# Second moments of h2: two products of 64 by 65 sums in place of one of 128 by 129

## The chip, the core and the metric

The program runs on one NeuronCore of a Trainium2 chip. The metric is the time of one execution on the device in microseconds (us). TensorE multiplies, VectorE, ScalarE and GpSimd work element by element, SyncE issues most transfers. TensorE is an array of 128 rows (the contraction) by 128 columns (the outputs of one pass), which can also be used in halves of 64 columns.

## What is computed

Two layers on x of shape (4, 256, 64, 64), in fp32. The first makes 49 weights for each pixel by a dilated 7x7 convolution and a 1x1 convolution, takes their softmax, and sums the 49 shifted copies of x with them. The second is a bottleneck block, with batch statistics in each normalisation:

```python
residual = x
h = relu(bn(conv(x, w1), g1, b1))            # 1x1, 256 -> 64 channels
h = relu(bn(conv(h, w2, pad=1), g2, b2))     # 3x3,  64 -> 64 channels: "h2"
h = bn(conv(h, w3), g3, b3)                  # 1x1,  64 -> 256 channels
return relu(h + residual)
```

The third normalisation needs mean and variance of each of 256 channels of conv(h2, w3). They follow from the sums of h2 over all pixels and from the sums of products of each two of its 64 channels (the second moments): the variance of channel c is w3_c' M w3_c less the square of the mean. Only these 64 by 64 sums and 64 plain sums are wanted.

## The kernel before

The kernel makes the weights of the first layer in transformed form (to about 450 us of the span), then turns them into banded matrices and applies them to x on TensorE, writing the result y to memory (`y_dram`) and taking conv1's statistics on the way (line 785 is conv1). Next come the 3x3 convolution (lines 952 and 964), the part that is changed here, and the output stage.

**h2 in SBUF.** `h2` has 128 partitions: 64 channels of one group of pixels in partitions 0 to 63 (the half with a = 0), the same channels of another group in 64 to 127. It is cut into 16 blocks of 128 partitions by 512 columns.

**The loop over blocks** (lines 1021 to 1036). For each block:
- ScalarE applies scale, shift and relu in place (line 1023).
- TensorE transposes it in four pieces j of 128 columns (line 1026) into a PSUM tile `pturn`, so that pixels lie on partitions.
- VectorE copies the tile (line 1028) into one of three buffers `ht`, each of four pieces of 129 columns. The 129th column holds ones, written once by GpSimd (line 1001).
- TensorE multiplies each piece by itself (line 1030): stationary operand 128 columns, moving operand all 129, summed in the PSUM tile `moments` over all 64 pieces. An fp32 product is done in two passes, so that the profile shows 128 matmuls with a weight load each.

Of the 128 by 129 sums, the two diagonal blocks of 64 by 64 (one for each half) and the last column (the plain sums) are used; the blocks that pair one half with the other are not read.

**After the loop.** Two VectorE copies take the diagonal blocks into `prod` (line 1046), one instruction scales the sums (line 1047), and a product with w3 (line 1049) with a few small steps (lines 1050 to 1059) gives scale and shift for the output. In the output stage TensorE computes conv3 (line 1013), VectorE adds y (line 1070), ScalarE applies the relu (line 1075), and SyncE's queue writes the result.

**Order.** The stages up to conv1 have hand-written orders on some engines; the loop here has none, and a scheduler orders each engine's instructions from its own estimates. It puts TensorE's work as: 4 transposes, 4 products of block 0, and then five times 12 transposes and 12 products, three blocks at a time, as many as `ht` has buffers. VectorE and ScalarE take their blocks in order. PSUM has 8 tiles in the pool `pb`, of which `moments` holds one.

Of the kernel before, what the change touches and what calls it, by code (L numbers as in the profile page):

```python
# [44 lines left out]
ALU = mybir.AluOpType  # L45
# [3 lines left out]
P = 128  # L49
B, C, H, W = 4, 256, 64, 64  # L50
# [5 lines left out]
MID = 64  # L56
# [37 lines left out]
def conv_seq_kernel(ctx: ExitStack, tc: tile.TileContext, xp, xt, w1, b1, w2t, b2, m1t, g1, be1,  # L94
                    m2t, g2, be2, m3t, g3, be3, z, mask, pavg, out, ydram):
    nc = tc.nc
    def pool(stack, name, bufs, space=None, **kw):
        if space is not None:
            kw["space"] = space
        return stack.enter_context(tc.tile_pool(name=name, bufs=bufs, **kw))  # L100
# [396 lines left out]
    for g in range(2):  # L497
        half = slice(g * MID, (g + 1) * MID)
# [7 lines left out]
    outer = pool(ctx, "outerp", 1).tile([P, OUTER], F32, name="outer")  # L506
# [155 lines left out]
    o = 4 * XT  # L662
# [3 lines left out]
    o = OUTER - NH1  # L666
# [33 lines left out]
    o = NH1  # L700
# [3 lines left out]
    o = 7 * C * 4  # L704
# [123 lines left out]
    def small(*shape):  # L828
        o, n = n_small[0], 1
        for d in shape:  # L830
            n *= d
        n_small[0] += n
        assert n_small[0] <= ARENA
        t = arena[:, o : o + n]
        return t.rearrange("p (n v) -> p n v", v=shape[1]) if len(shape) > 1 else t
# [159 lines left out]
    ops = [outer[:, 2048 * i : 2048 * (i + 1)].rearrange("p (r w) -> p r w", w=W) for i in range(4)]  # L995
    o = 4 * 2048

    ht = [outer[:, o + 4 * (P + 1) * i : o + 4 * (P + 1) * (i + 1)].rearrange("p (j c) -> p j c", j=4) for i in range(3)]
    o += 12 * (P + 1)
    for t in ht:  # L1000
        nc.gpsimd.memset(t[:, :, P:], 1.0)
    yins += [outer[:, o + 1024 * i : o + 1024 * (i + 1)] for i in range(6)]
    yins += [arena[:, 1024 * i : 1024 * (i + 1)] for i in range(7)]
    for n in range(19, len(parts)):
# [14 lines left out]
    moments = pb_.tile([P, 512], F32, tag="pb", name="moments")  # L1019
    blocks = [(slot, i, q) for slot in range(2) for i in range(2) for q in range(Q)]  # L1020
    for n, (slot, i, q) in enumerate(blocks):
        v = h2[:, slot, q, 512 * i : 512 * (i + 1)]
        nc.scalar.activation(v, v, AF.Relu, bias=sh2, scale=sc2)
        pt = pb_.tile([P, 512], F32, tag="pb", name="pturn2")
        for j in range(4):
            nc.tensor.transpose(pt[:, j * P : (j + 1) * P], v[:, j * P : (j + 1) * P], ident)  # L1026
        t = ht[n % 3]
        nc.vector.tensor_copy(t[:, :, :P], pt.rearrange("p (j c) -> p j c", j=4))
        for j in range(4):
            nc.tensor.matmul(  # L1030
                moments[:, : P + 1],
                t[:, j, :P],
                t[:, j, :],
                start=(n == 0 and j == 0),
                stop=(n == len(blocks) - 1 and j == 3),
            )
    prod = small(MID)
    sums = small(1)
    w3p = small(C)[:MID]
# [1 line left out]
    mv3 = small(NH, 2)  # L1041
    sq3 = small(NH, 1)
    nc.gpsimd.memset(one, 1.0 / (B * H * W))
    for g in range(2):
        half = slice(g * MID, (g + 1) * MID)
        nc.vector.tensor_copy(prod[half], moments[half, half])
    nc.vector.tensor_scalar(sums, moments[:, P : P + 1], 1.0 / (B * H * W), None, ALU.mult)
    pt = pb_.tile([P, 512], F32, tag="pb", name="pprod")
    nc.tensor.matmul(pt[:MID, :C], prod, w3m, start=True, stop=True)
    nc.vector.tensor_tensor(w3p, pt[:MID, :C], w3m[:MID], ALU.mult)  # L1050
# [1 line left out]
    for half in range(NH):  # L1052
        c = slice(half * P, (half + 1) * P)
# [8 lines left out]
    blocks = [(slot + 2 * g, i, half) for slot in range(2) for i in range(2) for half in range(NH) for g in range(2)]  # L1062
    for k, (b, i, half) in enumerate(blocks):
        o = ops[k % 4]

        n = 256 if k in (0, len(blocks) - 1) else 512
# [68 lines left out]
```

## Time and profile before

| what | value |
| --- | --- |
| median of 3 runs | 800.9 us (800.84 to 802.21) |
| profiled execution: its time, its span | 799.53 us, 797.6 us |
| TensorE, VectorE, ScalarE, GpSimd busy, of the span | 91%, 72%, 37%, 9% |
| granted TensorE clock, mean | 0.971 |
| products of line 1030: number, busy | 128, 16.7 us |
| transposes of line 1026: number, busy | 64, 9.4 us |
| copies of line 1028: number, busy | 16, 10.2 us |
| relus of line 1023: number, busy | 16, 11.4 us |
| first and last product of the moments start at | 720.7 us, 744.1 us |

Busy time counts an engine as busy from the start of an instruction to its end; matmuls overlap, so what one of them takes of TensorE is read from the spacing of their starts. "PEld" is the weight load that goes ahead of each matmul. In a row of the profile, 128*64 after the operation means 128 rows and 64 columns of the array, and 128x512 the partitions and elements of the operand.

### The profile page before, as it was taken

The page shows a single profiled execution, that of the slowest core. Times are in us where ns is not written, and L with a number is a line of the kernel's source. Part 1 is how long each engine was busy: PE and PEld are TensorE (multiplying, and loading weights), DVE is VectorE, ACT ScalarE, POOL GpSimd, SP SyncE. Part 2 cuts the span into 40 slices and gives each one's busy share as a digit, 9 for nine tenths or more (in the row PEclk, how much of TensorE's full clock was granted, in tenths as well). Part 3 has the DMA queues.
Part 4 walks back from the last instruction along what each step waited for, and adds up shares of the span by engine and source line. Part 5 has one row for each costly group of instructions (what it writes and reads, how often), then busy time and mean ns, then how long its engine had stood idle before and what let it go on. Part 6 is the DMA issues. An engine that isn't in the chain of part 4 may idle for free.

```text
span 797.6 us, 10675 instructions
## 1 busy us (share of the span) xinstructions
PE 729.1 (91%) x4080; PEld 590.2 (74%) x4080; DVE 574.6 (72%) x682; ACT 297.7 (37%) x594; POOL 75.7 (9%) x143
## 2 busy tenths in 40 slices
PE   0949999999999999988999999999999979979996
PEld 0938977888888888867888888988887854438742
DVE  4489989999666999999999867233341337663697
ACT  4640155112551101110111158434442446345497
POOL 3210010001000020000002113222222200000000
PEclk9979999999999999998999999999999998998997
DMA  7941089913898886210210013666766669361298
GB/s 290 373 162 41 0 292 297 382 57 126 287 341 349 311 307 233 71 41 11 60 37 16 2 57 101 202 220 212 229 234 212 212 238 342 108 196 39 85 391 367
DMA packets 59236, 150.24 MB, mean 188 GB/s; under 512 B 7346, under 2 KB 35634, under 8 KB 55090
## 3 DMA queue, kind: packets, MB, share of 16 engines
q1 hardware_dynamic: 51216, 141.11, 49.7%
q10 hardware_dynamic: 7970, 8.45, 3.0%
q8 instruction: 32, 0.52, 0.3%
q14 instruction: 18, 0.15, 0.1%
HBM read 93.81 MB, written 55.74 MB: 188 GB/s over the span
## 4 chain that ended last, share of the span: by engine, by line
PE 72%; DVE 15%; ACT 5%; DMA 4%; issue 2%; POOL 0%; SPq 0%; ACTq 0%; DVEq 0%; POOLq 0%
PE acc L262 42%; PE acc L752 13%; DVE arena L151 9%; PE acc L785 4%; PE pconv L964 3%; PE pdirect L952 3%; DVE arena L1070 3%; PE acc L566 2%; PE moments L1030 2%; PE acc L325 2%; ACT outer L1075 1%; DMA outer<-in_xt_dram 1%; ACT arena L573 1%; DMA w1raw<-in_w_dram 1%; PE pturn L1026 1%
## 5 line engine op out<-in xcount | busy, mean ns | idle before, releaser
L262 PE MATMUL acc<-arena 128*128 128x343 f32 (+3 forms) x2000 | 380.2, 353 | 20.5 <-DVE arena L151 20.5
L262 PEld LDWEIGHTS acc<-arena 128*128 128x128 f32 x2000 | 321.6, 192 | 78.1 <-issue 15.7
L151 DVE SCALAR_TENSOR_TENSOR arena<-arena 128x1024 f32<-128x1024 f32 (+7 forms) x192 | 290.5, 1554 | 24.7 <-PE acc L262 14.2
L752 PEld LDWEIGHTS acc<-arena,outer 128*128 128x128 f32 x1024 | 116.0, 193 | 11.3 <-issue 10.1
L752 PE MATMUL acc<-arena,outer 128*128 128x128 f32 x1024 | 118.8, 277 | 3.1 <-issue 2.9
L793 DVE BATCH_NORM_STATS2 st<-acc 128x6 f32<-128x512 f32 x16 | 11.2, 699 | 68.2 <-PE acc L785 68.0
L286 ACT COPY sv<-acc 128x392 f32<-128x392 f32 x40 | 19.1, 484 | 99.2 <-PE acc L262 87.3
L170 ACT COPY stage<-raw 128x128 f32<-128x128 f32 x128 | 43.6, 415 | 23.9 <-DMA raw<-in_xp_dram 23.5
L325 PE MATMUL acc<-powers,w1raw 128*128 128x196 f32 (+1 forms) x196 | 45.3, 394 | 6.6 <-DMA w1raw<-in_w_dram 5.0
L325 PEld LDWEIGHTS acc<-powers,w1raw 128*128 128x128 f32 x196 | 44.5, 314 | 7.1 <-issue 7.0
L590 ACT COPY outer<-acc 128x784 f32<-128x784 f32 x8 | 6.5, 812 | 101.8 <-PE acc L262 101.8
L1013 PE MATMUL pconv<-arena,w3m 64*128 64x512 f32 (+1 forms) x144 | 43.0, 587 | 0.6 <-DVE arena L1070 0.6
L123 ACT COPY outer<-outer 64x2048 f32<-64x2048 f32 x15 | 28.4, 1895 | 38.4 <-DMA outer<-in_xt_dram 38.4
L151 DVE SCALAR_TENSOR_TENSOR outer<-outer 128x784 f32<-128x784 f32 (+2 forms) x47 | 36.8, 835 | 3.6 <-ACT outer L906 3.6
L1013 PEld LDWEIGHTS pconv<-arena,w3m 64*128 64x128 f32 x144 | 20.7, 185 | 21.9 <-DVE arena L1070 16.0
L1075 ACT ACTIVATE outer<-arena 128x512 f32<-128x512 f32 (+1 forms) x58 | 34.7, 695 | 1.3 <-DVE arena L849 1.1
L773 DVE COPY bks<-acc 128x256 f32<-128x256 f32 x32 | 11.3, 417 | 32.5 <-PE acc L752 32.5
L1070 DVE SCALAR_TENSOR_TENSOR arena<-pconv,arena 128x512 f32<-128x512 f32 (+1 forms) x58 | 34.3, 667 | 0.0
L124 POOL COPY outer<-outer 64x1792 f32<-64x1792 f32 x15 | 25.1, 1676 | 95.5 <-DMA outer<-in_xt_dram 80.1
L607 ACT COPY acc<-bks 128x392 f32<-128x392 f32 x40 | 18.5, 488 | 40.7 <-DVE outer L592 33.8
L573 ACT COPY arena<-acc 128x512 f32<-128x512 f32 x52 | 27.1, 708 | 14.8 <-PE acc L566 14.4
L964 PE MATMUL pconv<-outer,arena 128*128 128x512 f32 x72 | 31.1, 592 | 0.0
(143 smaller groups left out, 627.7 us busy)
## 6 DMA issues: line engine op xcount, KB each, us to landing
raw<-in_xp_dram SPq DMA_DIRECT2D x36, 608.0 KB, 5.3
outer<-in_xt_dram SPq DMA_DIRECT2D x17, 896.0 KB, 6.3
out_dram<-outer SPq DMA_DIRECT2D x14, 1024.0 KB, 4.5
arena<-y_dram SPq DMA_DIRECT2D x25, 512.0 KB, 7.9
fsort_dram<-stage SPq DMA_DIRECT2D x2, 4864.0 KB, 14.7
arena<-fsort_dram SPq DMA_DIRECT2D x8, 1216.0 KB, 10.0
y_dram<-outer SPq DMA_DIRECT2D x16, 512.0 KB, 5.4
aside_dram<-sv ACTq DMA_DIRECT2D x40, 196.0 KB, 5.7
```

Of the source, the lines that this page charges most:

```text
L123: nc.scalar.copy(t[:MID], x[MID:])
L151: nc.vector.scalar_tensor_tensor(out, in0, scalar, in1, ALU.mult, ALU.add)
L170: (last if last and k + a == 2 else nc.scalar.copy)(d[:, k, :, PLACE[b], 2 * a : 2 * a + 2, i : i + count], raw[:, lo : lo + 4 * count - 3 ...
L262: nc.tensor.matmul(acc[i][d][:, o : o + (hi - lo) * K], xi[:, i, CW * w : CW * w + CW, :].rearrange("p x t -> p (x t)"), u[i][:, lo * K : ...
L325: nc.tensor.matmul(pw[:, o : o + n], w1raw[:, :, u * K7 + v], powers[:, u, :n], start=(u == 0), stop=(u == K7 - 1), skip_group_check=True,)
L573: nc.scalar.copy(dst, src)
L752: nc.tensor.matmul(dst[:, :: NT - 1] if edge else pts[c][:, o : o + 128], x[:, i, half * P : (half + 1) * P], amat[:, b % 2, :, c, blocks, ...
L785: nc.tensor.matmul(pt[a * MID : (a + 1) * MID, :], w1m[:, n, :], ys[a, n][:, 512 * i : 512 * i + 512], start=(n == 0), stop=(n == NH - 1), ...
L964: nc.tensor.matmul(m[k], wu[:, k, j, :], vs[k][:, g, j : j + R, :], start=(j == 0), stop=(j == 1))
L1013: nc.tensor.matmul(pt[:, :n], w3m[part, half * P : (half + 1) * P], h2[part, slot, q, lo : lo + n], start=True, stop=True)
L1070: nc.vector.scalar_tensor_tensor(v, conv3(b, q, i, half, lo, n), sc3[:, half : half + 1], v, ALU.mult, ALU.add)
L1075: nc.scalar.activation(dst, v.rearrange("p (r w) -> p r w", w=R), AF.Relu, bias=sh3[:, half : half + 1])
```

## The change

Each piece of `ht` is cut into two groups g of 64 columns with a column of ones each (4 pieces of 2 by 65 columns in place of 4 by 129). For each piece and group there is one product: the group's 64 columns are the stationary operand, its 65 the moving one, and the sums go to the 64 partitions of `moments` that belong to the group, which is one half of the array's columns. The sums are then 128 by 65: the diagonal blocks lie one below the other, the plain sums in column 64, and one copy takes them. The products double in number, from 64 to 128 (from 128 passes to 256).

```diff
-    ht = [outer[:, o + 4 * (P + 1) * i : o + 4 * (P + 1) * (i + 1)].rearrange("p (j c) -> p j c", j=4) for i in range(3)]
-    o += 12 * (P + 1)
+    HT = 8 * (MID + 1)
+    ht = [outer[:, o + HT * i : o + HT * (i + 1)].rearrange("p (j g c) -> p j g c", j=4, g=2) for i in range(3)]
+    o += 3 * HT
     for t in ht:
-        nc.gpsimd.memset(t[:, :, P:], 1.0)
+        nc.gpsimd.memset(t[:, :, :, MID:], 1.0)
...
         t = ht[n % 3]
-        nc.vector.tensor_copy(t[:, :, :P], pt.rearrange("p (j c) -> p j c", j=4))
+        nc.vector.tensor_copy(t[:, :, :, :MID], pt.rearrange("p (j g c) -> p j g c", j=4, g=2))
         for j in range(4):
-            nc.tensor.matmul(
-                moments[:, : P + 1],
-                t[:, j, :P],
-                t[:, j, :],
-                start=(n == 0 and j == 0),
-                stop=(n == len(blocks) - 1 and j == 3),
-            )
+            for g in range(2):
+                nc.tensor.matmul(
+                    moments[g * MID : (g + 1) * MID, : MID + 1],
+                    t[:, j, g, :MID],
+                    t[:, j, g, :],
+                    start=(n == 0 and j == 0),
+                    stop=(n == len(blocks) - 1 and j == 3),
+                    skip_group_check=True,
+                )
...
-    for g in range(2):
-        half = slice(g * MID, (g + 1) * MID)
-        nc.vector.tensor_copy(prod[half], moments[half, half])
-    nc.vector.tensor_scalar(sums, moments[:, P : P + 1], 1.0 / (B * H * W), None, ALU.mult)
+    nc.vector.tensor_copy(prod, moments[:, :MID])
+    nc.vector.tensor_scalar(sums, moments[:, MID : MID + 1], 1.0 / (B * H * W), None, ALU.mult)
```

## The prediction

> **What bounds the kernel now.** I read the chain of work that ended last first, in the stretch from the normalisation of h2 to the output stage, since the change touches only the loop over the 16 blocks there. Columns: start in us, length in us, what.
>
> ```profile
> 720.73 2.09 PE moments L1030 x8
> 722.81 2.20 PE pturn L1026 x12
> 725.01 2.68 PE moments L1030 x24
> 727.69 1.31 PE pturn L1026 x12
> 729.00 2.86 PE moments L1030 x24
> 731.86 1.31 PE pturn L1026 x12
> ...
> 741.50 2.87 PE moments L1030 x24
> ```
>
> TensorE alone carries this stretch. After one block by itself the order is three blocks of transposes (12 instructions), then the three products (24: an fp32 product of j is two passes, 64 products give 128 records). One turn is 731.86 - 727.69 = 4.17 us: 1.31 of transposes (109 ns each), 2.68 of products (112 ns each, as in the third row) and 0.18 of waiting. The last turn ends at 744.37. The groups of the same stretch say what one instruction costs and how idle the others are:
>
> ```profile
> L1030 PE MATMUL moments<-outer 128*128 128x129 f32 x128 | 16.7, 288 | 0.9 <-DVE outer L1028 0.9
> L1030 PEld LDWEIGHTS moments<-outer 128*128 128x128 f32 x128 | 15.6, 199 | 1.9 <-DVE outer L1028 1.3
> L1028 DVE COPY outer<-pturn 128x512 f32<-128x512 f32 x16 | 10.2, 685 | 14.5 <-PE pturn L1026 14.5
> L1046 DVE COPY arena<-moments 64x64 f32<-64x64 f32 x2 | 0.4, 223 | 1.9 <-PE moments L1030 1.8
> ```
>
> VectorE has 0.685 us a block and idles 14.5 us; ScalarE's 16 relus end at 729.3. The view of busy time by stretches adds the clock and what lies behind:
>
> ```profile
> 718.70:724.50 5.80, 4.89 (x21) 4.49 (x22) 1.38 (x2) 5.80 (x10) 0.00 (x0) 0.50 0.19 74
> 724.50:744.40 19.90, 19.86 (x173) 19.07 (x171) 8.83 (x15) 4.79 (x7) 0.00 (x0) 1.00 0.01 1
> 744.40:751.10 6.70, 5.54 (x34) 4.22 (x36) 4.29 (x17) 2.04 (x6) 0.00 (x0) 1.00 0.00 0
> 751.10:779.10 28.00, 28.00 (x92) 12.98 (x88) 28.00 (x45) 27.84 (x44) 0.00 (x0) 1.00 0.89 360
> ```
>
> Busy time is PE, weight loads, VectorE, ScalarE, GpSimd; then clock, DMA share, GB/s. TensorE runs at half clock up to 724.50. The queues are empty (share 0.01) from then to 751, so no transfer waits inside this stage, and the output stage behind it starts from its results: what the stage gives up reaches the end.
>
> **Does the array run two half-width products at once?** The timeline of line 785, whose products write 64 array columns each in alternate halves, answers:
>
> ```profile
> 519.77 0.59 PE L785 MATMUL acc<-outer,w1m 128*64 128x512 f32 x1
> 519.78 0.59 PE L785 MATMUL acc<-arena,w1m 128*64 128x512 f32 x1
> 520.20 0.59 PE L785 MATMUL acc<-outer,w1m 128*64 128x512 f32 x1
> 520.21 0.59 PE L785 MATMUL acc<-arena,w1m 128*64 128x512 f32 x1
> 520.73 0.49 PE L752 MATMUL acc<-arena,outer 128*128 128x128 f32 x2
> ```
>
> The halves start within 10 ns of each other, and each starts again 0.43 us later for 512 columns: 0.84 ns a column in both at once. The last row prices the return to the full array: 520.73 - 520.20 = 0.53, of which 0.43 is streaming, so about 97 ns pass before the next weight load begins. The way in, from line 752 at 647.35 to line 785's first load at 647.56, is 0.204 for 128 columns (0.107): 97 ns too.
>
> **What the Trainium skill says.** (1) TensorEngine Tiling (Array Packing), Key Properties: tiles load and multiply in parallel, and changing the tiling mode drains the engine. The trace agrees with both, and the drain is 97 ns here. (2) TensorE: Matmul & The Clock Gate, LDWEIGHTS: the load goes with the number of columns, P/1.2 ns. Line 785's 64-column loads take 139 ns against 192 for 128 in line 1030: 53 less, as stated. (3) Same page, Back-to-back issue gap: a floor of about 25 ns from start to start, 62 ns per matmul with hardware decode off. No run here shows so small a matmul, but lines 1030's 109 to 112 ns for a load and a matmul rule out 62 for each of the two. (4) Same page, The HAM clock gate: the clock follows activity in free-running windows of 3.4 us. The trace agrees: half clock ended at 724.50, after a window that was busy throughout.
>
> **The change, part by part.** The view of instruction order adds one thing that the diff doesn't show: the turn becomes M8 T1 M16 T3 T4 T4 (M products, 8 to a block; T transposes). One transpose of the next block slips in between the products, four times over.
>
> *Product.* A block has 16 passes, 8 in each half. A pass is 65 x 0.84 = 54 ns; line 1030 takes 112 for 129 x 0.84 = 108, so I add 4: **58 ns**. Its load (64 columns, 54 ns) hides under the pass before, as in line 785. A block: 8 x 58 = 0.46 us against 8 x 112 = 0.90. Bounds: not below 54; from above, two passes in turn, 116. The queue must take 32 instructions in 0.46 us, 14 ns each. The densest evidence is three pairs of semaphore instructions of the transposes, each pair 125 ns apart with 8 instructions between: 16 ns at most, some 9 when the 51 ns of the first is taken off. So 58 stands, with 70 possible.
>
> *Switches.* Into products: drain 97 + an uncovered load of 54 = 0.15 us. Back: 97 + 107 = 0.20. A turn has two of each.
>
> *A turn.* Products of the first block at 0 to 0.46; switch 0.20, one transpose 0.11, switch 0.15: 0.93. Two blocks to 1.86. VectorE's copies for them end about 0.55 and 1.24, so they hold nothing up. Switch 0.20, three transposes 0.33, eight 0.87: 3.26. Then either the switch (0.15) or VectorE's copy: in the trace 1.055 us pass from a block's last transpose (727.86) to its product's load (728.91), which gives 3.39. So **3.41 against 4.17: 0.76 less**, four times: 3.0. The old 0.18 of waiting has gone into the drain.
>
> *Start.* Block 0 is done about 0.45 us sooner, but the 12 transposes after it then run nearly all at half clock (218 ns), where now the last few run after 724.50 at 109. The next products begin at 724.78 instead of 724.85: 0.1 less.
>
> *End.* Three blocks follow the last transposes with no slot to fill, and VectorE is next in line: its third copy ends 1.24 after the first product, load at 1.30, product to 1.82. With the switch, 2.08 after the last transpose starts (741.24), against 744.19 - 741.24 = 2.95 now: 0.87 less.
>
> *Around it.* One copy of 128x64 for two of 64x64 (0.22 + 0.24): 0.23 less. Three GpSimd memsets of 8 columns for 4 (105 ns each, over by 714.7, five us ahead of the first copy), the copies' 8 runs for 4, sums read from another column: nothing; if the 8 runs cost 50 ns each, only the end would see 0.1. The product of line 1049 has 64 columns already and follows without a switch. No DMA is moved.
>
> Sum: 3.0 + 0.1 + 0.87 + 0.23 = **4.2 us less**. The profiled execution took 799.53 (span 797.6); 795.3 after. The median before, 800.9, lies 1.4 above the profiled one, so **796.7**. A measurement of this kernel tells about 0.2%, 1.6 us, from no change: the bounds are 799.3 and 802.5.
>
> **Rivals.**
> - *A denser stream isn't fed.* Steps of 70 to 85 ns make a block 0.56 to 0.68: up to 0.2 x 16 = 3.2 us back, **798.3 to 799.9**. For it: 32 instructions where 16 were. Against: 9 to 16 ns each. 0.11.
> - *The clock comes late.* The window to 724.50 now holds a drain and 0.65 us of products instead of an unbroken stream. Should it not count as busy, 3.4 us more run at half clock: 1.7 back, **798.4**. The view by stretches shows full clock following a window that was 93% busy (55.4 to 58.9) and not one of 57% (656.2 to 659.65); I get 89%. 0.10.
> - *Slower: the halves take turns.* If 65-column passes don't overlap as 512-column ones do, a block takes 16 x 58 = 0.93, nothing is won, and the switches stand: a turn is 2.78 + 1.31 + 0.71 = 4.80, 0.63 more. 4 x 0.63 + 0.1 at the end + 0.3 at the start - 0.23 = 2.7 more, **803.6**. It decides from the step at which 3 x 8 steps + 2.02 reach 4.17: 90 ns. For it: nothing that short is in the trace. Against: the 10 ns between the halves of line 785. 0.13. With the loads uncovered too (16 x 108 a block), a turn is 7.2 and the time some **816**: 0.04.
>
> **Numbers.** The forecast has 0.62, itself from 795.3 to 798.2 (a step of 54 to 66). Faster: 0.62 + 0.10 and a third of the 0.11, 0.76; same: the rest of it, 0.07; slower: 0.13 + 0.04 = 0.17. The range from 795.3 to 800.6 leaves out the two slower cases, and a little for a forecast that falls below it.
>
> **What would show it.** Products as 128*64 128x65 x256, two starts within 10 ns and 58 ns a step; a turn of 3.4; VectorE's copy 0.69 still; output stage of the same length. A step over 90 ns, or full clock only at 727.9, would make it wrong.

## The result, and the profile after

The median after is **796.4 us** (6 runs, 794.59 to 797.52) against 800.87 before (6 runs); the ratio is 0.9935, with a 95% interval from 0.9917 to 0.9953, so 3.8 to 6.6 us less. The forecast was 796.7. The profiled execution took 796.58, with a span of 794.3.

The chain of waits of the kernel after, in the stretch shown of before (start in us, length in us, what; lines 1026 and 1030 are now 1027 and 1032):

```profile
722.94 1.14 PE moments L1032 x16
724.08 2.49 PE pturn L1027 x12
726.57 0.62 PE moments L1032 x16
727.19 0.26 PE pturn L1027
727.45 1.08 PE moments L1032 x32
728.53 1.35 PE pturn L1027 x11
729.88 0.62 PE moments L1032 x16
...
739.81 1.82 PE moments L1032 x48
741.65 0.23 DVE arena L1047
```

TensorE still carries the stretch, but a turn (from one group of 16 passes after 11 transposes to the next) is 729.88 - 726.57 = 3.31 us where it was 4.17. The one transpose between the products is there.

The groups of the same stretch, as for the kernel before:

```profile
L1027 PE MATMUL pturn<-ident,arena 128*128 128x128 f32 x64 | 10.7, 313 | 2.5 <-ACT arena L1024 2.5
L1032 PE MATMUL moments<-outer 128*64 128x65 f32 x256 | 10.4, 232 | 0.9 <-DVE outer L1029 0.9
L1029 DVE COPY outer<-pturn 128x512 f32<-128x512 f32 x16 | 10.2, 686 | 10.6 <-PE pturn L1027 10.6
L1032 PEld LDWEIGHTS moments<-outer 128*64 128x64 f32 x256 | 8.9, 143 | 2.7 <-issue 1.4 <-DVE outer L1029 0.7
```

There are twice as many passes, and they take less time: 10.4 us of busy time for 16.7. The copy into 8 runs of 64 costs 686 ns, as the copy into 4 runs of 128 did (685). How the passes lie is seen in TensorE's timeline:

```profile
730.04 0.46 PE L1032 MATMUL moments<-outer 128*64 128x65 f32 x10
730.43 0.33 PE L1027 MATMUL pturn<-ident,arena 128*128 128x128 f32 x1
730.69 0.40 PE L1032 MATMUL moments<-outer 128*64 128x65 f32 x6
```

Single records in the trace: passes start at 726.610 and 726.618, 726.669 and 726.676, 726.728 and 726.736. Two halves start 8 ns apart, and each starts again 58.5 ns later. The rows above show a switch: the last two passes begin at 730.272 and 730.279, the load of the transpose at 730.43, the next products at 730.69.

Last, busy time by stretches (PE, weight loads, VectorE, ScalarE, GpSimd, then clock, DMA share, GB/s), cut where the clock rises and where the stage ends:

```profile
720.90:726.17 5.27, 4.34 (x30) 3.85 (x31) 1.53 (x3) 5.27 (x8) 0.00 (x0) 0.50 0.25 94
726.17:741.65 15.48, 15.44 (x292) 13.34 (x290) 8.69 (x14) 5.32 (x8) 0.00 (x0) 1.00 0.02 4
...
748.00:776.00 28.00, 28.00 (x91) 12.99 (x88) 28.00 (x45) 27.84 (x45) 0.00 (x0) 1.00 0.89 360
```

Half clock lasted 5.2 us from the first transpose (720.95), where it had lasted 5.7 before: the clock was not late. The output stage is as it was, only earlier.

**The stage against the whole.** I count the stage from the first transpose to the first copy out of `moments`: 25.64 us before, 20.70 after. With the copies up to the product of line 1049 it is 26.24 and 20.98, so 5.26 less. The spans of the two profiled executions differ by only 3.3, because the code ahead of the stage, which is the same in both, took 2.2 us longer in the second (first transpose at 718.76 and 720.95). Over the profiled kernels here that leave the code ahead of it alone, that first transpose starts anywhere from 717.8 to 724.0. What an experiment does is therefore read from its stage first and from its median second.

### The profile page after: what moved, and what is told of

It is laid out like the page before. It is cut to its first block, busy times and chain, and to the rows that moved or that the text cites. A ratio compares the mean times of both kernels' runs of the same rounds, so it can differ in the third digit from the quotient of the medians.

```text
span 794.3 us, 10929 instructions
## 1 busy us (share of the span) xinstructions
PE 725.6 (91%) x4208; PEld 585.4 (74%) x4208; DVE 574.2 (72%) x681; ACT 297.7 (37%) x594; POOL 75.3 (9%) x143
## 4 chain that ended last, share of the span: by engine, by line
PE 71%; DVE 16%; DMA 5%; ACT 4%; issue 2%; POOL 0%; SPq 0%; ACTq 0%; DVEq 0%; POOLq 0%
PE acc L262 42%; PE acc L752 12%; DVE arena L151 8%; DVE arena L1071 4%; PE acc L785 4%; PE pconv L964 3%; PE pdirect L952 3%; DMA outer<-in_xt_dram 2%; PE acc L566 2%; PE acc L325 2%; DMA w1raw<-in_w_dram 1%; PE pturn L1027 1%; ACT arena L573 1%; PE moments L1032 1%; DMA raw<-in_xp_dram 1%
```

## The experiments

The theory: two halves at once at 58 ns a step, and about 0.15 us for each change between full and half array. The main rival: the smaller product gains by itself.

**One half of the columns (e1).** The products keep their size, but both groups go to the same half.

```diff
-                    moments[g * MID : (g + 1) * MID, : MID + 1],
+                    moments[:MID, g * (MID + 1) : (g + 1) * (MID + 1)],
...
-                    start=(n == 0 and j == 0),
+                    start=(n == 0 and j == 0 and g == 0),
...
+        nc.vector.tensor_copy(prod[half], moments[:MID, o : o + MID])
```

> The 128 products of 64 by 65 stay, but both groups of a piece go to the same half of the array's columns (group 1 to columns 65 to 129 of the same PSUM partitions), so that they cannot run side by side; two copies bring the sums to their partitions. The stage is counted from the first transpose to the first copy out of moments: 25.64 us before, 20.70 after. Theory (the gain is two halves at once, 58 ns a step in each): one step of 58 ns after the other, a block 0.94 us, a stage of 26.9 us, about 803 us in all, slower than before by 1 to 3 us. Rival (the gain is the smaller product alone: shorter loads and streams): a stage of 20 to 21 us, 796 to 797 us, as after.

Measured: a stage of 27.09 us, a median of 802.72 against 801.44 beside it, ratio 1.0013 (0.999 to 1.0036). From its chain of waits:

```profile
726.37 2.95 PE moments L1032 x48
729.32 1.46 PE pturn L1027 x12
730.78 2.94 PE moments L1032 x48
```

48 passes take 2.95 us with the switch into them, where side by side they take 1.55 (e8 below). In the records a pass starts every 58.4 ns, one after the other: 2.80 us without the switch against 1.40, twice as long. A turn is 4.41, longer than the wide products' 4.17. The narrow product alone gains nothing; the whole of the gain is that two run at once. The scheduler gave this kernel two switches a turn, not four: its turn is 2.80 of products, 1.31 of transposes and 0.30 of switches, where before had 2.68, 1.31 and 0.18 of waiting.

**Half the moving operand (e2).** The kernel before, each product in two, 64 and 65 columns of the moving operand on the full array.

```diff
+            for g in range(2):
+                c = slice(g * MID, (g + 1) * MID + g)
                 nc.tensor.matmul(
-                    moments[:, : P + 1],
+                    moments[:, c],
                     t[:, j, :P],
-                    t[:, j, :],
+                    t[:, j, c],
```

> The kernel before, with each product cut in two along the moving operand only (64 and 65 columns), all 128 columns stationary in both. Theory (the narrow product gains by its half-width weight load, which alone lets a pass go below 107 ns): each of the 256 passes waits for a load of 128 columns, 107 to 112 ns a pass, a block 1.76 us in place of 0.90; a stage of some 39 us and 814 us in all. Rival (a short moving operand is enough): 58 ns a pass, a stage of 25.6 us and 801 us, as before.

Measured: a stage of 41.26 us, a median of 817.74, ratio 1.0189 (1.0166 to 1.0212). At full clock 48 passes take 5.48 us. In the records they start 112 ns apart, for 54 ns of streaming:

```profile
738.82 5.48 PE moments L1032 x48
744.31 1.32 PE pturn L1026 x12
...
L1032 PEld LDWEIGHTS moments<-outer x256: 186/192/333, 725.4 to 764.4; 128*128 128x128 f32 x128
```

A stream as short takes 58.4 ns in e1 behind a load of 64 columns, so here the weight load of 128 columns sets the pass. So the half-width load is needed too, but e1 shows that it isn't enough. The stage is 2.3 us over the 39 expected. Of these the clock accounts for 1.7: it stayed at half for 9.2 us from the first transpose, in before for 5.7 (see the last section).

**The order (e3, e4, e8).** e3 and e4 write TensorE's order out; e8 is e3 with the second of each three copies on ScalarE. `turn2(n)` is relu, transposes and copy of a block, `multiply(n)` its products.

```diff
+    with tc.manual_schedule(engines={mybir.EngineType.PE}):
+        for do, n in [(turn2, 0), (multiply, 0)] + [(f, 3 * k + m) for k in range(5) for f in (turn2, multiply) for m in (1, 2, 3)]:   # e3 and e8
+        for do, n in [(f, n) for m in range(19) for f, n in ((multiply, m - 3), (turn2, m)) if 0 <= n < 16]:   # e4
+            do(n)
...
+        copy = nc.scalar.copy if n % 3 == 2 else nc.vector.tensor_copy   # e8
```

> The kernel after, with TensorE's order written out: three blocks of transposes, three of products, so two switches of the tiling a turn in place of four. Theory (a switch costs 0.15 us, but VectorE's copies are next in line: the third is ready 1.24 us after the first product starts): 0.30 of switches saved a turn and about as much waited for the copies; a turn of 3.2 to 3.4 us against 3.31, a stage of 20.4 us, within 0.5 us of after (796.0). Rival (only the number of switches counts): a turn of 3.01 us, a stage of 19.5 us, 795.2.

> The kernel after, with TensorE's order written out: after three blocks of transposes one block of products, one of transposes, in turn: six switches of the tiling for three blocks in place of four, and every copy done two blocks ahead. Theory (0.15 us for each switch, nothing else): a block takes 0.44 + 0.47 + 0.30 = 1.21 us, three 3.6 us; a stage of 21.5 us, 797.2 us in all. Rival (switches cost nothing much, and waiting for VectorE is what is left): 0.9 to 1.0 us a block, a stage of 18 us, 794.

> The order in threes written out, and the second of each three copies on ScalarE, which has nothing to do from the middle of the stage on. Theory (in threes the products wait for VectorE's third copy): the waits go, a turn is 24 x 58.5 ns + 12 x 109 + 0.30 = 3.02 us in place of 3.25; a stage of 19.0 us in place of 20.28, 1 us less in all. Rival (the turn of 3.25 is TensorE's own): the turn stays at 3.2 us or more.

The chains of waits: of e3, a turn without a wait and one with it; of e8, two turns without a wait and the products of one with it; of e4, one block:

```profile
729.70 1.55 PE moments L1037 x48
731.25 1.46 PE pturn L1029 x12
732.71 1.79 PE moments L1037 x48
734.50 1.46 PE pturn L1029 x12
```

```profile
724.53 1.55 PE moments L1038 x48
726.08 1.46 PE pturn L1029 x12
727.54 1.55 PE moments L1038 x48
729.09 1.46 PE pturn L1029 x12
730.55 0.62 PE moments L1038 x16
731.18 1.15 PE moments L1038 x32
```

```profile
728.41 0.59 PE pturn L1029 x4
729.00 0.62 PE moments L1037 x16
729.61 0.59 PE pturn L1029 x4
```

| kernel | switches a turn | turn, us | stage, us | ratio to before |
| --- | --- | --- | --- | --- |
| after | 4 | 3.31 | 20.70 | 0.9935 |
| e3, threes | 2 | 3.25 (the first 3.01) | 20.28 | 0.992 (0.9891 to 0.9948) |
| e8, threes, a copy on ScalarE | 2 | 3.01 (one of 3.24) | 19.52 | 0.9923 (0.9889 to 0.9957) |
| e4, singles | 6 | 3 x 1.20 = 3.61 | 21.37 | 0.9947 (0.992 to 0.9974) |

Without waits a turn should be 24 x 58.5 ns + 12 x 109 ns = 2.71 us and 0.15 for each switch: 3.01 for two, 3.31 for four, 3.61 for six. e8, after and e4 lie on that line. e3 lies 0.24 above it in all turns but the first, and e8 takes those 0.24 away by a copy on another engine: in threes the products wait for VectorE's second and third copies, which costs 0.11 and 0.13 us (1.79 us for 48 passes in place of 1.55). The scheduler's transpose between the products had filled that wait at the price of two switches, which come to about the same. The stage of e8 is 0.5 above the 19.0 expected, for two reasons. In one turn the products waited 0.23 for ScalarE's copy, which stood behind a relu and ended at 731.12. And e3 had only four waits to lose, in three turns and at the end. By their ratios the four kernels can't be told apart, so the verdicts rest on the turns.

**Fewer switches (e6, e7), beside after (e5).** 12 buffers `ht` and long groups; e7 has the wide products of before in the same order and as many buffers. `n % 3` becomes `n % 12` for the buffers.

```diff
-    ht = [outer[:, o + HT * i : o + HT * (i + 1)].rearrange("p (j g c) -> p j g c", j=4, g=2) for i in range(3)]
+    ht = [
+        outer[:, k : k + HT].rearrange("p (j g c) -> p j g c", j=4, g=2)
+        for k in [o + HT * i for i in range(3)] + [HT * i for i in range(9)]
+    ]
...
+        for do, n in [
+            (f, n)
+            for f, lo, hi in (
+                (turn2, 0, 10), (multiply, 0, 5), (turn2, 10, 16), (multiply, 5, 10), (multiply, 10, 16)
+            )
+            for n in range(lo, hi)
+        ]:
+            do(n)
```

> The kernel after, unchanged, on the chip of the runs beside it: a stage (first transpose to first copy out of moments) of 20.5 to 21.0 us, 4 to 5 us less than the kernel before in all.

> The kernel after with 12 buffers ht in place of 3 (9 in the memory of the output tiles, not yet in use) and TensorE's order written out: 10 blocks of transposes, 5 of products, 6 of transposes, 11 of products: three switches in the whole stage in place of 18, copies well ahead until the last. Theory (what is left of the stage is the switches and the waits for VectorE's copies): a stage of 17.9 us, 2.8 less than after, 793.6 us in all. Rival (the halves' overlap rests on the short bursts, or the transposes and copies take the time back at the start, at half clock): a stage of 20 us or more, no gain on after.

> The kernel before (products of 128 by 129) with the same 12 buffers and the same order as the kernel of the run beside it. Tells what the order and the buffers give without the halves. Theory (the wide products have no switches to save, only the 0.18 us waits, and lose 2.6 us to the half clock as before): a stage of 24.1 us, 1.5 less than before, some 799.4 us in all; so that the halves are worth 6.2 us of a stage in this order, against 4.9 in the order of the kernel after. Rival (the order, not the halves, makes the gain): a stage within 1 us of the narrow kernel's.

Measured: e5 a stage of 20.81 and a ratio of 0.9926 (0.9901 to 0.9952); e6 17.59 and 0.9913 (0.9881 to 0.9945); e7 23.96 and 0.9988 (0.9971 to 1.0006). The chain of e6, whole, and of e7:

```profile
721.14 7.01 PE pturn L1032 x40
728.15 2.48 PE moments L1040 x80
730.63 2.77 PE pturn L1032 x24
733.40 5.31 PE moments L1040 x176
```

```profile
717.81 7.01 PE pturn L1032 x40
724.83 4.47 PE moments L1039 x40
729.29 2.62 PE pturn L1032 x24
731.91 9.84 PE moments L1039 x88
```

In the same order and with the same buffers the halves are worth 23.96 - 17.59 = 6.4 us of the stage (6.2 were expected): 80 passes in 2.48 us against 40 in 4.47, and the one switch back to transposes (2.77 against 2.62) costs 0.15. The order and buffers alone give the wide products 1.7, of which about 0.5 is due to the clock: in e7 it rose 4.7 us after the first transpose, in before 5.7. So with its 19 switches (the expectation has 18) and waits the kernel after keeps 4.9 of those 6.4.

**The idle start (e11, e12), beside after and e6 (e9, e10).** e11 is after with 40 idle products ahead of the stage; e12 has them with 12 buffers and an order of 3, 5 and 8 blocks.

```diff
-    sc2, sh2 = from_sums(sums2, bn12[:, 2:3], bn12[:, 3:4])
...
+        for n in range(40):
+            if n == 30:
+                sc2, sh2 = from_sums(sums2, bn12[:, 2:3], bn12[:, 3:4])
+            nc.tensor.matmul(warm[:, :P], w3m[:, :P], w3m[:, P:], start=True, stop=True)
```

> The kernel after once more, beside the three runs that follow, on the chip that they use: a stage of 20.5 to 21.0 us, 0.990 to 0.995 of the kernel before.

> The kernel with 12 buffers and three switches once more, since its stage was 3.1 us shorter than after's in the profile and its median only 0.9 us lower. Theory (the stage's gain reaches the end; the medians differ by the noise of the stages ahead of it): a stage of 17.6 us, a ratio to before 0.003 to 0.004 below that of after. Rival (the order loses elsewhere what it gains in the stage): the same ratio as after.

> The kernel after with 40 products of 128 by 128 of w3 with itself, whose sums nothing reads, on TensorE in the time in which it waits for the end of the 3x3 convolution's statistics: 30 (60 passes, 6.7 us) before the product of line 867 and 10 after it. Theory (the first 5 us of the stage run at half clock for the idle time before; it costs 2 us): the clock stays full, a stage of 18.6 us in place of 20.7, 2 us less in all. Rival (the half clock costs little, since ScalarE's relus at 0.71 us a block pace the start): a stage within 0.5 us of 20.7.

> Both: the 40 products that keep the clock up, 12 buffers, and an order of 3, 5 and 8 blocks (transposes, then products of each), five switches. Theory: a stage of 16.0 us, 1.6 below the kernel with 12 buffers alone and 4.7 below after, 791 to 792 us in all. Rival (relus and copies bind): a stage of 17 us or more.

| kernel | stage, us | median, us | ratio to before |
| --- | --- | --- | --- |
| e9, after | 20.92 | 795.42 | 0.9924 (0.9897 to 0.995) |
| e10, 12 buffers | 18.12 | 792.12 | 0.9866 (0.9835 to 0.9897) |
| e11, idle products | 18.83 | 798.5 | 0.994 (0.9922 to 0.9958) |
| e12, both | 16.02 | 795.77 | 0.9912 (0.9883 to 0.9941) |

The granted clock was 1.00 from the first idle product to the end of the stage in e11 and e12, and both stages are what was expected, 18.83 for 18.6 and 16.02 for 16.0: the half clock at the start costs the kernel after 2 us. The stage of e10 is 0.5 longer than that of e6, which is the same kernel: its clock rose 6.1 us after the first transpose, that of e6 4.9.

But as kernels e11 and e12 failed, in the main by an error of mine. From the chain of e11:

```profile
715.05 6.70 PE warm L1012 x60
721.74 0.13 PE pm L867 x2
724.33 0.67 PE pturn L1032 x4
```

60 passes last 6.7 us, and the product of line 867, which the whole stage waits for, stands behind them. The last product of the 3x3 convolution had started at 714.45, and from that one to the first transpose 9.88 us pass in place of 7.22 in e9. The time I had filled was counted from 708.74, where the chain of before leaves TensorE, and not from its last product at 711.55. The stage gains 2.1 on e9 and the way to it loses 2.7. Another 0.9 is lost behind the stage: from the product of line 1049 to the end of the span e11 and e12 took 53.28 and 53.16 us, the other kernels 52.3 to 52.6. The engines finish as early as in e9 after that product, but the last write whose landing the trace shows took 4.6 and 4.5 us in place of 3.6; why stays open. Whether half as many passes before line 867 would pay wasn't tried.

The version with 12 buffers has a lower ratio than after in both its trials: 0.9913 and 0.9866, against after's 0.9926 and 0.9924 beside it, with a stage 3.2 and 2.8 us shorter. Against before both intervals are clear; against after the intervals meet, and that it is faster rests on the stage.

## Why the prediction was right

The stage gained 5.26 us where 4.2 was forecast, and the median moved by 4.5, with an interval of 3.8 to 6.6. That the median came within 0.3 us of the forecast is in part luck. The mechanism and the order of the turn came out as forecast; the sizes of some terms did not.

The terms of the sum, each from where the products really stream (their first load done) in the records of both traces:

| term | predicted, us less | measured, us less | from to, before; after |
| --- | --- | --- | --- |
| start, to the products of block 1 | 0.1 | 0.49 | 718.76 to 724.85; 720.95 to 726.56 |
| four turns | 3.0 | 3.43 | 724.85 to 741.52; 726.56 to 739.80 |
| end, to the first copy out | 0.87 | 1.02 | 741.52 to 744.40; 739.80 to 741.65 |
| copies, to line 1049 | 0.23 | 0.32 | 744.40 to 745.00; 741.65 to 741.93 |
| sum | 4.2 | 5.26 | |

- **The step of 58 ns** was right: 58.5. The Trainium skill (TensorEngine Tiling (Array Packing), Key Properties) has tiles working in parallel; line 785 gave the two rates that the estimate needed, and they hold for passes eight times shorter. The forecast's own range, 795.3 to 798.2, is wider than the steps of 54 to 66 ns named with it: 128 steps of 4 ns less or 8 more are 796.2 to 797.7.
- **The switch into products**, 0.15, was right. The drain that the Trainium skill names in the same section was forecast at 97 ns and is 94 here (a last transpose starts at 726.300 and streams 0.107, the next load starts at 726.501), and e8, after and e4 fit 0.15 on the mean of both ways.
- **The switch back** was mis-sized: 0.15, not 0.20. I gave the transposes' load 107 ns. A transpose that follows a switch lasts 329 ns and another 272, so its load leaves 57 uncovered. The trace of before had it: line 1026's loads take 141 ns where line 1030's take 192 for as many columns. With the drain that makes 0.15. Two of these a turn are the 0.10 between 3.41 and 3.31, and 0.4 in four turns.
- **The end**: VectorE's copies follow each other at 0.60 us, not 0.69 (728.167, 728.775, 729.373 in the trace of before): an instruction's length isn't its pitch. The third copy is done 0.18 earlier than I had it, which covers the difference of 0.15. Of the 0.32 from there to line 1049, 0.23 is the copy saved; the rest is a shorter gap before that product, 0.04 for 0.14.
- **The start** was mis-sized by 0.4. The clock rose 5.2 us after the first transpose in one execution and 5.7 in the other; 0.52 us more at full clock is worth 0.26. That depends on where the clock's window falls and isn't owed to the change. And the first switch back, at half clock, took 0.19 us (last pass at 723.765, its streaming 0.11, transposes stream from 724.065) where I had allowed some 0.4; at half clock that is worth another 0.1.
- **Nothing hid the gain**: the output stage and what lies between took 52.59 us before and 52.34 after, counted from line 1049 to the end of the span. What the stage gave up arrived at the end.

Of the rivals, the halves that take turns are excluded by the 8 ns and by e1, which shows what that would have cost: 27.09 us with two switches a turn, where the working behind 803.6 comes to about 28.6 with four. The stream was fed, at 14.6 ns for each of 32 instructions in 0.468 us. The clock was not late.

## What to carry to other kernels

Where only the diagonal blocks of a product are wanted, products of half the columns in alternate halves of the array run two at a time and save the other blocks, if the weight load is halved with them; count each change between full and half array at the drain plus the uncovered load, here 0.15 us at full clock, and group the work so that there are few. An engine that was hidden comes next in line (here VectorE's copies), and an order that fills its wait can cost as much as it saves. A gain of 5 us in a kernel whose unchanged part varies by as much is read from its stage in the trace.

## What the runs showed that I had not expected

- **Transposes alone raise the clock.** In e6 and e7 TensorE did nothing but transposes for 7.0 us, in e10 for 7.5, and full clock came 4.9, 4.7 and 6.1 us after the first, before the first product. The stretch of e6 up to the rise:

```profile
721.10:726.05 4.95, 4.91 (x23) 4.91 (x24) 3.11 (x5) 4.95 (x8) 0.00 (x0) 0.50 0.21 79
```

  The Trainium skill (TensorE: Matmul & The Clock Gate, Part 4: PE-mode transpose) says that full clock doesn't engage for transposes, which don't count as busy in the same way. These runs differ from that, and the measurement decides.
- **One run suggests that the time in which TensorE waits for weight loads doesn't count as busy.** In e2 the clock rose at 732.66, two windows after the products began at 725.45. By stretches, its busy time is full in both:

```profile
725.80:729.20 3.40, 3.40 (x18) 3.40 (x18) 0.00 (x0) 3.40 (x6) 0.00 (x0) 0.50 0.03 5
729.20:732.60 3.40, 3.40 (x18) 3.40 (x17) 2.08 (x3) 3.40 (x6) 0.00 (x0) 0.50 0.00 0
```

  In the first window a pass starts every 0.21 us and streams 64 columns at half clock, 0.11: half the time. In the second 2.5 of the 3.4 us are transposes (729.12 to 731.68), which stream throughout, and after it the clock rose. No run tests this by itself, so it is not shown.
